# Eight load buffers for the small convolutions, delta u written over u, and ScalarE seeding the sums' bank

## The chip, the cores and the metric

The kernel runs on one core of a Trainium2 chip. A core has five engines that run side by side, each with its own in-order queue: TensorE (matmuls; PE in the profile, with weight loads as PEld), VectorE (DVE), ScalarE (ACT), GpSimd (POOL) and SyncE (SP, which only issues transfers here). All transfers run on 16 DMA engines. The working memory is SBUF, matmuls write to PSUM[...], and scratch tensors lie in device memory (HBM). The metric is the device time of one execution in microseconds, lower is better.

## The reference, cut to what matters

Eight images of 384 channels and 32 x 32 pixels go through four layers. Layer 0 is a state space block over the 1024 pixels in sequence, run forwards and backwards with the same weights and added; with it goes a 3 x 3 convolution per channel. For each direction:

```python
u, z = split(x_norm @ in_proj.T)
u = silu(conv1d(u) + conv1d_b)            # four taps per channel, causal
dt, B, C = split(u @ x_proj.T)            # 24, 16 and 16 columns
delta = softplus(dt @ dt_proj + dt_b)
h = exp(delta * A) * h + (delta * u) * B  # step by step over the pixels, 16 states
y = (C * h).sum(states) + D * u
out = (y * silu(z)) @ out_proj.T
```

Layer 1 has two 1 x 1 convolutions around a 3 x 3 convolution per channel, linear attention and an MLP with GELU. Layers 2 and 3 have depthwise convolutions up to 13 x 13, for which all images are needed at once. Everything is float32.

## The kernel before, in words

**Stages.** Layers 0 and 1 run image by image in `_layers01`; layers 2 and 3 follow for all images together (`conv` in `tile_layers`, lines 282 to 372) and are not touched. For each image b there are three pieces: `front(b)` (lines 572 to 685) prepares the scan's inputs, `scan(b)` (lines 687 to 809) runs the recurrence, `layer1(b)` (lines 869 to 1077) is layer 1. The loop at the end interleaves `scan(b)`, `front(b + 1)` and `layer1(b - 1)`: after each of the scan's 48 rounds it takes as many steps of the other two as their share of cost asks for. Only the first front and the last `layer1` stand alone. The framework hands out buffers and puts the waits in; the order of each engine's queue comes from this interleaving, which the framework's planner may shift where it thinks an operand late.

**The front.** After a normalisation and the input projection, the 3 x 3 convolution (`conv3`, line 532) and the four-tap convolution (line 626 on) load shifted copies of their input from HBM: for each block of 128 channels four tiles of the tag `im`, one for 32 channels, each with three or four shifted copies in the partitions (L541 `lc_i` here and `dw_i` in layer 1, L637 `ut`). Four column groups of TensorE then work on the four tiles (L511). SyncE issues these loads, and in the same queue those of the scan. `N_IM` sets how many such tiles there are: six.

The four-tap convolution of both directions goes through silu into two tiles `uc` of the tag `a6` (L645), one for each direction, with three channel blocks each; seven tiles of that tag serve the whole of layers 0 and 1. For each channel block L666 and L670 then make delta (`dl`), and `deltas`, put off by a step or two, multiplies it with u (L676, into a tile `v` of the tag `t2`), sends both to HBM (L677, L678, on GpSimd's queue), adds the two directions' u (L679) and lets ScalarE scale the sum by D (L681, into `ud`, tag `t2`). `t2` is the general scratch tag of 128 x 512 tiles: eleven buffers, for the squares (L581), the projection's output, delta, v, ud, the MLP's hidden block `hm` (L1054) and others.

**The scan.** A unit is a direction, a half of the pixels and a block of 128 channels: 12 for each image. A unit has four rounds, each for four of the 16 states, and a round has two half rounds. In a half round ScalarE takes two exponentials (`da`, L768, four buffers), VectorE one product (`du`, L773) and two scans (`hs`, L785, eight buffers), and GpSimd one product with C (L794). TensorE sums over the states with a selection matrix, two rounds later (`sums`, line 724): four matmuls of 32 columns each (L728) into one PSUM bank `acc`, of which there is a single one, over the four rounds of a unit. Written in float32, a matmul is two instructions in the profile. In the first round an identity matmul (L733) adds `y0` to the bank: D u in the first direction, and in the second the first direction's result. At a unit's end the bank is copied out by ScalarE (L738) or multiplied with silu(z) by VectorE (L741). `y0`, the copy and z share three buffers of the tag `s2`.

Of the kernel before, what the change touches and what calls it, by code (L numbers as in the profile page):

```python
# [9 lines left out]
AF = mybir.ActivationFunctionType  # L10
# [10 lines left out]
HALF = 512  # L21
# [12 lines left out]
NR = NST // 4  # L34
IMG = (H + 2) * (W + 2)

N_A6, N_T2, N_S2, N_W, N_IM = 7, 11, 3, 4, 6
N_REP, N_DA, N_HS = 6, 4, 8
TP = H * (KP // 2)
PADW = KS // 2  # L40
# [334 lines left out]
def _layers01(tc, nc, B, xv, x2_d, dram, ident, mean_w, eps5, eps6, one, half, minus1, vec, bns, bnt,  # L375
# [12 lines left out]
    with ExitStack() as ctx:  # L388
# [26 lines left out]
        dlv = dl_d.rearrange("b d (c p) l -> b d p c l", p=P)  # L415
        vv = v_d.rearrange("b d (c p) l -> b d p c l", p=P)
# [45 lines left out]
        def t2(name):  # L462
            return sp.tile([P, HALF], FP, tag="t2", name=name, bufs=N_T2)
# [108 lines left out]
        def front(b):  # L572

            xn = []
            for h in range(2):
                cols = bass.ts(h, HALF)
                xh = a6(f"xi_{b}_{h}")
                nc.sync.dma_start(xh, xv[b][:, :, cols])
                sqs = [t2(f"sq_{b}_{c}_{h}") for c in range(NC)]
                for c in range(NC):  # L580
                    nc.scalar.activation(sqs[c], xh[:, c, :], AF.Square)  # L581
                rstd = rsqrt_mean(sqs, eps6, f"ms_{b}_{h}")
                t, mid = image6(f"xn_{b}_{h}")
                for c in range(NC):
                    nc.vector.scalar_tensor_tensor(
                        mid[c], rows(xh[:, c, :]), vec("norm_w", c), rows(rstd), ALU.mult, ALU.mult
                    )
                put_image(xn_d, b % 2, h, t, nc.gpsimd)
                xn.append(mid)
                yield 3  # L590
            uo = u_d[b % 2].rearrange("(c p) i -> p c i", p=P)
            for e in range(2):
                w = wtile(inproj_t[:, e * C : (e + 1) * C], f"win_{b}_{e}")
                for h in range(2):
                    for m in range(NC):
                        ps = psum(f"in_{b}_{e}_{m}_{h}")
                        dense(ps, w, m, xn[h])
                        t = t2(f"uz_{b}_{e}_{h}_{m}")
                        if e == 0:
                            nc.scalar.copy(t, ps)  # L600
                            nc.scalar.dma_start(uo[:, m, 3 + h * HALF : 3 + (h + 1) * HALF], t)
                        else:
                            nc.scalar.activation(t, ps, AF.Silu)
                            nc.scalar.dma_start(zv[b][:, m, bass.ts(h, HALF)], t)
                        yield 3


            t3 = tapw(taps3, f"t3_{b}")
            for h in range(2):
                for c in range(NC):  # L610
                    xr = t2(f"xr_{b}_{h}_{c}")
                    nc.sync.dma_start(xr, xv[b][:, c, bass.ts(h, HALF)])
                    ps = conv3(xn_d, b % 2, h, c, t3, f"lc_{b}_{h}_{c}")
                    lc = t2(f"lg_{b}_{c}_{h}")
                    nc.scalar.activation(lc, ps, AF.Sigmoid, bias=vec("dw_b0", c))

                    def local(h=h, c=c, lc=lc, xr=xr):
                        nc.vector.tensor_mul(rows(lc), rows(lc), xn[h][c])
                        nc.vector.scalar_tensor_tensor(xr, lc, rs, xr, ALU.mult, ALU.add)
                        nc.gpsimd.dma_start(x1v[b][:, c, bass.ts(h, HALF)], xr)  # L620

                    defer(1, local)
                    yield 3


            for h in range(2):
                cols = bass.ts(h, HALF)
                ucs = [a6(f"uc_{b}_{h}_{d}") for d in range(2)]
                for c in range(NC):
                    uts = []  # L630
                    for j in range(4):
                        ut = sp.tile([P, 18 * (W + 2)], FP, tag="im", name=f"ut_{b}_{h}_{c}_{j}", bufs=N_IM)
                        src = bass.AP(
                            u_d.tensor, u_d[b % 2, 32 * (4 * c + j), h * HALF].offset,
                            [[UL, 32], [1, 4], [1, HALF + 3]],
                        )
                        nc.sync.dma_start(ut[:, 0 : HALF + 3], src)  # L637
                        uts.append(ut)
                    for d in range(2):
                        ps = psum(f"c1_{b}_{h}_{c}_{d}")  # L640
                        col32(
                            ps, lambda j, i: t1[:, d * NG + 4 * c + j, :],
                            lambda j, i: uts[j][:, 3 * d : 3 * d + HALF], 1,
                        )
                        nc.scalar.activation(ucs[d][:, c, :], ps, AF.Silu, bias=vec("conv1d_b", c))  # L645
                    yield 2

                xd = t2(f"xd_{b}_{h}")
                ps = psum(f"xd_{b}_{h}")
                for k in range(NC):  # L650
                    for d in range(2):
                        nc.tensor.matmul(
                            ps[64 * d : 64 * d + 64, :], wx[:, k, :], ucs[d][:, k, :],
                            start=(k == 0), stop=(k == NC - 1), skip_group_check=True,
                        )
                nc.scalar.copy(xd, ps)
                for d in range(2):
                    lo = 64 * d + DTR
                    nc.scalar.dma_start(bc_d[b, d][:, cols], xd[lo : lo + 2 * NST, :])
                yield 3  # L660
                for c in range(NC):
                    dls = []
                    for d in range(2):
                        ps = psum(f"dt_{b}_{h}_{d}_{c}")
                        at = slice(64 * d, 64 * d + DTR)
                        nc.tensor.matmul(  # L666
                            ps, wdt[at, c * P : (c + 1) * P], xd[at, :], start=True, stop=True
                        )
                        dl = t2(f"dl_{b}_{h}_{d}_{c}")
                        nc.scalar.activation(dl, ps, AF.Softplus, bias=vec("dt_b", c))  # L670
                        dls.append(dl)

                    def deltas(h=h, c=c, dls=dls, ucs=ucs):
                        for d in range(2):
                            dl, t = dls[d], t2(f"v_{b}_{h}_{d}_{c}")
                            nc.vector.tensor_mul(t, dl, ucs[d][:, c, :])  # L676
                            nc.gpsimd.dma_start(dlv[b, d][:, c, bass.ts(h, HALF)], dl)  # L677
                            nc.gpsimd.dma_start(vv[b, d][:, c, bass.ts(h, HALF)], t)  # L678
                        nc.vector.tensor_add(ucs[0][:, c, :], ucs[0][:, c, :], ucs[1][:, c, :])  # L679
                        ud = t2(f"ud_{b}_{h}_{c}")  # L680
                        nc.scalar.activation(ud, ucs[0][:, c, :], AF.Copy, scale=vec("D", c))  # L681
                        nc.scalar.dma_start(udv[b][:, c, bass.ts(h, HALF)], ud)

                    defer(1, deltas)
                    yield 3

        def scan(b):
# [36 lines left out]
            def sums(k, r, hs, acc, y0, zt):  # L724
                d, h, c = units[k]
                cols = bass.ts(h, HALF)
                for j in range(4):
                    nc.tensor.matmul(  # L728
                        acc[32 * j : 32 * j + 32, :], selt, hs[j // 2][:, bass.ts(j % 2, HALF)],
                        start=(r == 0), stop=(r == NR - 1), skip_group_check=True,  # L730
                    )
                if r == 0:
                    nc.tensor.matmul(acc, ident, y0, start=False, stop=False, skip_group_check=True)  # L733
                if r < NR - 1:
                    return
                if d == 0:
                    yt = s2(f"yt_{b}_{h}_{c}")
                    nc.scalar.copy(yt, acc)  # L738
                    nc.scalar.dma_start(yfv[b][:, c, cols], yt)
                else:  # L740
                    nc.vector.tensor_mul(zt, acc, zt)  # L741
                    nc.gpsimd.dma_start(gv[b][:, c, cols], zt)
# [3 lines left out]
            acc = y0 = zt = nxt = None  # L746
            for k, (d, h, c) in enumerate(units):
                cols = bass.ts(h, HALF)
                second = k % (2 * NC) >= NC
                for r in range(NR):  # L750
                    if r == 0:
                        acc = accp.tile([P, HALF], FP, tag="acc", name=f"acc_{b}_{d}_{h}_{c}")
                        y0 = s2(f"y0_{b}_{d}_{h}_{c}")
# [9 lines left out]
                    for i in range(2):  # L763
                        dlt, vt = now[i]
                        da = sp.tile([P, 2 * HALF], FP, tag="da", name=f"da_{b}_{k}_{r}_{i}", bufs=N_DA)
                        for j in range(2):
# [3 lines left out]
                                scale=neg_a[:, g, r : r + 1],  # L770
# [435 lines left out]
```

## Time and profile before

The time is 5718.41 us, the median of 3 runs (5712.15 to 5722.47). The profiled execution spans 5739.7 us.

| Engine | Busy, us | Share of the span | Instructions |
|---|---|---|---|
| TensorE, matmuls | 4793.9 | 84% | 19550 |
| VectorE | 3602.0 | 63% | 3679 |
| ScalarE | 2886.6 | 50% | 3821 |
| GpSimd | 2872.7 | 50% | 1603 |

| Stage | Stretch, us | TensorE busy | VectorE | ScalarE | GpSimd |
|---|---|---|---|---|---|
| first front alone | 0 to 220 | 118.54 | 24.65 | 49.42 | 56.38 |
| scan of image 1 | 220 to 690 | 296.78 | 414.86 | 274.15 | 319.48 |
| scan of image 4 | 1870 to 2430 | 482.44 | 405.54 | 349.43 | 317.11 |
| scan of image 5 | 2430 to 2990 | 486.50 | 417.17 | 353.77 | 326.72 |
| last `layer1` alone | 4590 to 4960 | 311.25 | 30.12 | 72.32 | 10.72 |
| layers 2 and 3 | 4960 to 5740 | 739.74 | 131.01 | 100.65 | 158.51 |

The page's line of an engine in forty slices has one digit for each slice of 143 us, the busy share in tenths. An answer of waits reads "engine, line, what waited for it": the total in us, how often, and the longest. In the order of time a line has the start, the time taken, engine, source line, operation, output and inputs, the count, and in brackets how long the engine stood idle before it and what let it go. SPq and POOLq are the parts of those engines that issue transfers. Averages over the whole run hide that the stages have different limits, so each is read by itself.

### The profile page before, as it was taken

What the parts mean: (1) busy time and instruction counts of PE and PEld (TensorE: products, weight loads), DVE (VectorE), ACT (ScalarE), POOL (GpSimd) and SP (SyncE); (2) the same over time, 40 slices, a digit from 0 to 9 for tenths busy, and PEclk for the clock granted to TensorE, in tenths of its full rate; (3) what the DMA queues carried; (4) which work ended last, traced back from release to release, by engine and by line L of the source; (5) the groups of instructions that cost most, each with busy time, mean ns of one, the idle gap of its engine ahead of it and who ended that gap; (6) DMA issues with size and microseconds to landing.
All of it is one profiled execution on the core that took longest, in us unless ns stands there. A gap on an engine that the chain in (4) does not pass through costs nothing. (4 is left out here: it accounts for less than half of the span.)

```text
span 5739.7 us, 57345 instructions
## 1 busy us (share of the span) xinstructions
PE 4793.9 (84%) x19550; PEld 2100.7 (37%) x19550; DVE 3602.0 (63%) x3679; ACT 2886.6 (50%) x3821; POOL 2872.7 (50%) x1603
## 2 busy tenths in 40 slices
PE   4666579878898799779888997898878879899899
PEld 1121123322332243224323332332233224597498
DVE  0498887868887668676877785788578701111211
ACT  1555546764676368646774676467636612000211
POOL 3376665647755556565655574557456700110133
PEclk7786689988999899989999998899989989999999
DMA  9655575677567755764565477547644531466676
GB/s 297 220 181 166 175 238 175 224 195 225 175 219 217 208 170 190 173 214 129 182 213 181 139 184 204 171 148 190 180 135 133 128 88 50 105 162 162 192 165 151
DMA packets 528252, 1012.13 MB, mean 176 GB/s; under 512 B 60616, under 2 KB 196248, under 8 KB 527960
## 3 DMA queue, kind: packets, MB, share of 16 engines
q1 hardware_dynamic: 387952, 665.99, 39.2%
q0 software_dynamic: 71136, 248.53, 16.8%
q10 hardware_dynamic: 68872, 93.95, 5.0%
q8 instruction: 155, 2.54, 0.2%
q14 instruction: 137, 1.12, 0.1%
HBM read 763.86 MB, written 288.36 MB: 183 GB/s over the span
## 5 line engine op out<-in xcount | busy, mean ns | idle before, releaser
L794 POOL TENSOR_TENSOR hs<-hs,bct 128x1024 f32<-128x1024 f32 x768 | 2362.9, 3078 | 1160.7 <-DVE hs L785 659.6
L768 ACT ACTIVATE da<-dlt,neg_a 128x512 f32<-128x512 f32 x1536 | 1031.3, 714 | 864.1 <-DVE hs L785 780.0
L785 DVE TENSOR_TENSOR_SCAN hs<-da,carry,du 128x512 f32<-128x512 f32 x768 | 946.8, 1268 | 411.2 <-PE acc L728 228.1
L773 DVE TENSOR_TENSOR du<-vr,bct 128x1024 f32<-128x1024 f32 x768 | 1043.4, 1359 | 121.7 <-DMA vr<-v_d 74.7
L785 DVE TENSOR_TENSOR_SCAN hs<-da,du 128x512 f32<-128x512 f32 x768 | 900.9, 1208 | 187.5 <-ACT da L768 110.9
L728 PE MATMUL acc<-hs,selt 128*32 128x512 f32 x3072 | 725.2, 665 | 271.6 <-POOL hs L794 214.5
L1056 PE MATMUL mo<-hm,w 128*128 128x512 f32 x1152 | 557.3, 623 | 66.1 <-ACT hm L1054 42.9
L502 PE MATMUL mf<-ln,w 128*128 128x512 f32 x1152 | 554.9, 623 | 55.7 <-ACT dl L670 28.9
L768 ACT ACT_TABLE_LOAD x299 | 383.6, 1283 | 30.5 <-DVE hs L785 20.5
L728 PEld LDWEIGHTS acc<-hs,selt 128*32 128x32 f32 x3072 | 124.1, 114 | 683.7 <-POOL hs L794 351.8
L1056 PEld LDWEIGHTS mo<-hm,w 128*128 128x128 f32 x1152 | 213.6, 195 | 400.4 <-issue 242.0
L502 PEld LDWEIGHTS mf<-ln,w 128*128 128x128 f32 x1152 | 218.4, 198 | 381.1 <-issue 297.4
L502 PE MATMUL in<-xn,win 128*128 128x512 f32 x576 | 302.2, 658 | 39.5 <-ACT phi_k L866 35.0
L511 PE MATMUL dw<-dw_i,t3b 96*32 96x512 f32 x1152 | 243.4, 728 | 94.3 <-DMA dw_i<-h_d 94.0
L316 PE MATMUL cv_b<-xt_b,toep 128*64 128x256 f32 x2688 | 305.0, 389 | 14.4 <-DVE xt_b L298 14.4
L316 PE MATMUL cv_a<-xt_a,toep 128*64 128x256 f32 x2688 | 304.2, 388 | 9.2 <-DVE xt_a L298 9.2
L316 PEld LDWEIGHTS cv_b<-xt_b,toep 128*64 128x64 f32 x2688 | 282.6, 199 | 37.2 <-issue 16.8
L316 PEld LDWEIGHTS cv_a<-xt_a,toep 128*64 128x64 f32 x2688 | 282.3, 199 | 30.8 <-issue 10.2
L511 PE MATMUL lc<-lc_i,t 96*32 96x512 f32 x1152 | 218.1, 675 | 61.9 <-DMA lc_i<-xn_d 32.2
L1054 ACT ACTIVATE hm<-mf,biasf 128x512 f32<-128x512 f32 x192 | 131.6, 687 | 169.0 <-PE mf L502 167.4
L502 PE MATMUL op<-g,wo 128*128 128x512 f32 x288 | 149.7, 666 | 76.7 <-issue 42.6
L511 PE MATMUL c<-ut,t 128*32 128x512 f32 x768 | 175.2, 655 | 40.4 <-DMA ut<-u_d 37.7
(184 smaller groups left out, 5296.8 us busy)
## 6 DMA issues: line engine op xcount, KB each, us to landing
dlt<-dl_d SPq DMA_DIRECT2D x384, 256.0 KB, 4.4
vr<-v_d SPq DMA_DIRECT2D x384, 256.0 KB, 4.7
bct<-bc_d SPq DMA_DIRECT2D x256, 256.0 KB, 3.7
ut<-u_d SPq DMA_DIRECT2D x192, 257.5 KB, 5.4
lc_i<-xn_d SPq DMA_DIRECT2D x192, 228.8 KB, 5.0
dw_i<-h_d SPq DMA_DIRECT2D x192, 228.8 KB, 4.2
tp_d<-g_d POOLq DMA_DIRECT2D x64, 672.0 KB, 7.1
w<-w_d SPq DMA_DIRECT2D x64, 576.0 KB, 5.4
```

What stands on the lines that cost most here:

```text
L316: nc.tensor.matmul(ps[2 * H * e : 2 * H * (e + 1), 0:BW], tp[:, 2 * (g % (GB // 2)) + e, :, :, t].rearrange("p c j -> p (c j)"), rhs, star ...
L502: nc.tensor.matmul(ps, w[:, k, m * P : (m + 1) * P], rhs[k] if isinstance(rhs, list) else rhs[:, k, :], start=(k == 0), stop=(k == NC - 1),)
L511: nc.tensor.matmul(ps[32 * j : 32 * j + 32, :], lhs(j, i), rhs(j, i), start=(i == 0), stop=(i == taps - 1), skip_group_check=True,)
L728: nc.tensor.matmul(acc[32 * j : 32 * j + 32, :], selt, hs[j // 2][:, bass.ts(j % 2, HALF)], start=(r == 0), stop=(r == NR - 1), skip_group ...
L768: nc.scalar.activation(da[:, bass.ts(j, HALF)], dlt[:, bass.ts(j, HALF)], AF.Exp, scale=neg_a[:, g, r : r + 1],)
L773: nc.vector.tensor_mul(pairs(du), pairs(vt), bct[r][:, 0:1, :].to_broadcast([P, 2, HALF]),)
L785: nc.vector.tensor_tensor_scan(t[:, s][:, way], da[:, s][:, way], du[:, s][:, way], k_c if second else 0.0, ALU.mult, ALU.add,)
L794: nc.gpsimd.tensor_mul(pairs(t), pairs(t), bct[r][:, 1:2, :].to_broadcast([P, 2, HALF]))
L1054: nc.scalar.activation(hm, ps, AF.Gelu, bias=biasf[:, NC * i + f, :])
L1056: nc.tensor.matmul(acc[m], wb[:, f, m * P : (m + 1) * P], hm, start=(i == 0 and f == 0), stop=(i == FF // C - 1 and f == NC - 1),)
```

## The change

Three edits, which share the same memory: two tiles of 2048 bytes a partition go and two of 2448 come.

- The convolutions' loads get eight buffers and not six, enough for two whole convolutions. The scratch tag `t2` gives up two, from eleven to nine.
- delta u is written over u in the tile `uc`, and the store to HBM reads it there; no tile `v` is taken. As u is then gone, the sum of the two directions' u is taken first, into the tile `ud`, which ScalarE scales in place.
- D u (or the first direction's result) reaches the sums' bank by a ScalarE copy ahead of the selection matmuls, which then all add to the bank. The identity matmul stays in the very first unit alone, with the start flag, ahead of the selection matmuls.

```diff
-N_A6, N_T2, N_S2, N_W, N_IM = 7, 11, 3, 4, 6
+N_A6, N_T2, N_S2, N_W, N_IM = 7, 9, 3, 4, 8
...
                     def deltas(h=h, c=c, dls=dls, ucs=ucs):
+                        ud = t2(f"ud_{b}_{h}_{c}")
+                        nc.vector.tensor_add(ud, ucs[0][:, c, :], ucs[1][:, c, :])
                         for d in range(2):
-                            dl, t = dls[d], t2(f"v_{b}_{h}_{d}_{c}")
-                            nc.vector.tensor_mul(t, dl, ucs[d][:, c, :])
-                            nc.gpsimd.dma_start(dlv[b, d][:, c, bass.ts(h, HALF)], dl)
-                            nc.gpsimd.dma_start(vv[b, d][:, c, bass.ts(h, HALF)], t)
-                        nc.vector.tensor_add(ucs[0][:, c, :], ucs[0][:, c, :], ucs[1][:, c, :])
-                        ud = t2(f"ud_{b}_{h}_{c}")
-                        nc.scalar.activation(ud, ucs[0][:, c, :], AF.Copy, scale=vec("D", c))
+                            v = ucs[d][:, c, :]
+                            nc.vector.tensor_mul(v, dls[d], v)
+                            nc.gpsimd.dma_start(dlv[b, d][:, c, bass.ts(h, HALF)], dls[d])
+                            nc.gpsimd.dma_start(vv[b, d][:, c, bass.ts(h, HALF)], v)
+                        nc.scalar.activation(ud, ud, AF.Copy, scale=vec("D", c))
                         nc.scalar.dma_start(udv[b][:, c, bass.ts(h, HALF)], ud)
...
             def sums(k, r, hs, acc, y0, zt):
                 d, h, c = units[k]
                 cols = bass.ts(h, HALF)
+                if r == 0 and b == 0 and k == 0:
+
+                    nc.tensor.matmul(acc, ident, y0, start=True, stop=False, skip_group_check=True)
+                elif r == 0:
+                    nc.scalar.copy(acc, y0)
                 for j in range(4):
                     nc.tensor.matmul(
                         acc[32 * j : 32 * j + 32, :], selt, hs[j // 2][:, bass.ts(j % 2, HALF)],
-                        start=(r == 0), stop=(r == NR - 1), skip_group_check=True,
+                        start=False, stop=(r == NR - 1), skip_group_check=True,
                     )
-                if r == 0:
-                    nc.tensor.matmul(acc, ident, y0, start=False, stop=False, skip_group_check=True)
                 if r < NR - 1:
                     return
                 if d == 0:
```

## The prediction

> **What bounds the kernel now.** I read the page's slices first, then a table of 100 us stretches, then the waits of each engine, and last the order of time at two places.
>
> ```profile
> PE   4666579878898799779888997898878879899899
> DVE  0498887868887668676877785788578701111211
> ACT  1555546764676368646774676467636612000211
> ```
>
> Forty slices of 143 us. The last eight belong to the large convolutions, which this change does not touch. From slice 2 to 32 (220 to 4590 us) the scan of eight images runs beside other work. In its first image (220 to 690 us) VectorE is full (414.86 us busy of 470) and TensorE is not (296.78), so VectorE sets the pace. In each later image, some 560 us long, TensorE is busy for about 486 us and VectorE for about 420: neither is full over the whole image.
>
> ```profile
> 2000.00:2100.00 100.00, 97.17 (x346) 46.73 (x345) 60.24 (x52) 56.75 (x87) 51.42 (x28) 0.98 0.47 151
> 2400.00:2500.00 100.00, 71.26 (x231) 26.77 (x230) 71.43 (x86) 52.05 (x75) 56.81 (x39) 0.85 0.77 187
> 2600.00:2700.00 100.00, 96.98 (x319) 39.95 (x318) 66.97 (x62) 66.89 (x93) 53.39 (x21) 0.93 0.44 133
> 2800.00:2900.00 100.00, 88.59 (x262) 29.37 (x257) 84.09 (x76) 73.09 (x87) 68.70 (x34) 0.95 0.65 200
> ```
>
> The columns are TensorE, its weight loads, VectorE, ScalarE, GpSimd, the granted clock, the DMA share and GB/s. About four of the six stretches of an image look like the first, third and fourth rows (TensorE 88 to 97%, the bound); the start of an image looks like the second: nobody is full, and waits set the time. These are the waits that the change touches:
>
> ```profile
> PE dw L511 <- DMA dw_i<-h_d: 94.0, 41, 9.9
> PE c L511 <- DMA ut<-u_d: 37.7, 21, 11.1
> PE lc L511 <- DMA lc_i<-xn_d: 32.2, 11, 10.2
> PE mf L502 <- ACT dl L670: 28.9, 6, 7.0
> PE mf L502 <- ACT uc L645: 22.0, 7, 5.0
> PE acc L728 <- ACT yt L738: 28.4, 10, 7.2
> PE acc L728 <- DVE zr L741: 28.4, 16, 6.7
> ```
>
> The numbers are total us, times and the longest. The first three are TensorE waiting for convolution loads (163.9 us), the next two for ScalarE, the last two for the one bank of the sums to come free.
>
> [...] The trace has 562 to 587 ns for the sums' copy on L738; that is used. [...] in the trace no copy line carries a table load. [...] the multiply on L676 takes 660 ns at least and 2856 at most.
>
> **Part 1, the identity matmul (L733).**
>
> ```profile
> L733 PE MATMUL acc<-y,ident x192: 592/697/1222, 233.0 to 4576.3; 128*128 128x512 f32 x192
> ```
>
> Each of the 96 is two instructions; 95 pairs go. The timeline around 2319 us has a pair at 2318.95 and the next matmul at 2320.01, so one is worth 1.06 us of TensorE: 95 x 1.06 = 101 us. The first image holds 11 of them under a full VectorE, worth nothing there; 84 x 1.06 = 89 us lie in images two to eight. TensorE sets the pace in about 0.6 of those: **-53 us** (ends 0 and -89).
>
> In their place stand 95 ScalarE copies of 0.585 us (L738's median), 56 us. ScalarE is half busy and sits 780.0 us before the exponentials of L768 waiting for VectorE, so I cost the copies' own time at nothing. The new waits are another matter. The copy must wait for the bank: ahead of it in ScalarE's queue, in direction 0, is its own copy out (L738); in direction 1 it waits for VectorE's multiply on L741. Queued behind it are the exponentials and the evictions of the other layers. The exponentials are up to four tiles ahead of the scan, so a wait of one half round (3.8 us from scan to scan at 2500 us) starves nobody. On the other side the four sums matmuls now wait for ScalarE to reach the copy. Where TensorE already waits for the bank today (10 + 16 times in the list above) it will wait longer: 0.6 us more for the copy in the 16, and in the 10 also for up to two exponential pairs of 1.33 us: 16 x 0.6 + 10 x 3.3 = 43 us of TensorE, mostly at the starts of images where it is not full: **+20 us** (ends 0 and +43; if ScalarE is late in many more of the 95 units, 95 x 1 us more).
>
> **Part 2, eight load buffers.** A convolution takes four loads. With six buffers the third and fourth load of the next convolution wait until the one before has been computed, and a load lands some 4 us after its issue. At 2503.72 us SyncE issues six loads, from then on four at a time as TensorE lets go. With eight, two whole convolutions are in flight. SyncE's queue is in order, and behind a held load stand the scan's own: SyncE waits 200.9 us for L541 on lc, 135.4 on dw, 116.3 for L637, and VectorE loses 74.7 us to late vr and, between 1270 and 4115 us, 25.9 us to late bct loads. Of the 163.9 us of TensorE waits 105.7 lie between 600 and 4580 us (76.0 + 25.4 + 4.3); half of that comes through to the end, since VectorE is 70 to 85% busy there: -50. The first 220 us run at a DMA share of 0.85 and gain little, the last image's own convolution after 4590 us about 10, its 9.9 us wait: **-60 us** (ends -20 and -110).
>
> **Part 3, delta u in the place of u, and the sum first.**
>
> ```profile
> 2339.98 3.44 DVE L676 TENSOR_TENSOR v<-dl,uc 128x512 f32<-128x512 f32 x2
> 2343.34 0.68 DVE L679 TENSOR_TENSOR uc<-uc,uc 128x512 f32<-128x512 f32 x1
> 2344.05 0.72 ACT L681 ACTIVATE ud<-uc,pk 128x512 f32<-128x512 f32 x1 [6.86 <-DVE uc L679]
> 2346.82 2.84 PE L502 MATMUL mf<-ln,w 128*128 128x512 f32 x6 [3.63 <-ACT uc L645]
> 2348.84 1.28 DVE L785 TENSOR_TENSOR_SCAN hs<-da,carry,du 128x512 f32<-128x512 f32 x1 [3.63 <-ACT da L768]
> ```
>
> ScalarE's D u (L681) stands in its in-order queue until VectorE has done two multiplies and the sum; TensorE (3.63 us) and the scan (3.63 us) then wait for what is queued behind it. With the sum first, ScalarE is let go two multiplies earlier: 3.4 us here, 2 x 0.96 = 1.9 us by the mean L676 between 600 and 4580 us. 37 such waits x 1.9 = 70 of the 120.6 us that L681 waits. What reaches TensorE are the waits of L502 mf above, 28.9 + 22.0 = 51 us; half of them: **-25 us** (ends 0 and -70). The instructions themselves stay the same in number and shape: nothing.
>
> **Part 4, nine scratch tiles and not eleven.** The deltas take 3 scratch tiles a block and not 5, so nine last three blocks and eleven lasted 2.2. At the turn of an image this matters:
>
> ```profile
> 1273.13 0.61 ACT L581 ACTIVATE sq<-xi 128x512 f32<-128x512 f32 x1
> 1283.64 0.54 POOL L678 DMA_DIRECT2D v_d<-v  x1 [10.28 <-DMA x_d<-xx]
> 1295.70 0.63 ACT L581 ACTIVATE sq<-xi 128x512 f32<-128x512 f32 x1 [21.95 <-DMA ud_d<-ud]
> 1296.97 1.22 DVE L785 TENSOR_TENSOR_SCAN hs<-da,du 128x512 f32<-128x512 f32 x1 [23.05 <-ACT da L768]
> ```
>
> The second square finds no scratch tile until stores leave, the stores stand in GpSimd's queue, which is held by the stores of x_d, and ScalarE holds the scan 23.05 us. Three squares and one more tile after 15 delta tiles in 11 need 8 of them back; after 9 in 9 they need 4. The stall stays in part, since GpSimd is held as before. ScalarE's square waits are 41.5 + 19.2 us: **-20 us** (ends 0 and -45). Against it: everywhere else two tiles fewer, and u's tiles, seven for all users, are held until the store of v has landed and not only until the sum; the load of the next image stands behind that in SyncE's queue. No row shows either; between 0 and one landing of some 5 us at each of 7 turns: **+10 us** (ends 0 and +40).
>
> **Sum.** -53 + 20 - 60 - 25 - 20 + 10 = -128 us. The waits overlap: a stall that TensorE loses in part 2 or 3 lets it run into VectorE, 75% busy, sooner. I take 0.8 of it, -103: 5718 - 103 = **5615 us**.
>
> **Rivals.**
> (a) Another engine takes over. VectorE loses no work; an image is some 560 us with VectorE at 420 us busy, 465.81 and 481.55 in the second and third. Then waits only change hands (TensorE's from loads and ScalarE to GpSimd's product on L794, today 214.5 us) and a third of the sum is left, -43, with part 1's new waits at their upper end (23 more): about 5698. For it: in the first image this is so already. Against it: four stretches in six have TensorE at 88% or more.
> (b) The stalls are chains, and taking the head of each frees all engines at once: the parts at two thirds of their far ends, (89 + 110 + 70 + 45) x 2/3 = 209, less 30 for the new waits: about 5540. For it: at 2348 and 1297 us TensorE, VectorE and ScalarE stand together. Against it: the DMA share of 0.6 to 0.7 bounds how much earlier loads can land.
> (c) Slower. ScalarE late at the copies in all 95 units (95 x 1 us), u's tiles and scratch at their ends (+40), and only half of the gains of parts 2 to 4 (-52) and a third of part 1 (-18), with the 43: -52 - 18 + 95 + 40 + 43 = +108; at half of that, about 5770. For it: ScalarE's queue is in order and carries table loads (1283 ns) between the exponentials and the other layers' functions, and it is 70 to 80% busy in the later half of an image, so it can be behind TensorE there. Against it: TensorE is behind all others in just that half.
>
> **How the numbers follow.** Forecast 0.58, (a) 0.18, (b) 0.12, (c) 0.12. Faster by over 0.2% (11 us): forecast, (b) and most of (a), 0.84; within it: the rest of (a) and the mild end of (c), 0.05; slower 0.11. The range has the forecast, half of (b) and all but the end of (a): 5540 to 5705.
>
> **What would show each step.** Part 1: the row of L733 at 2 instructions, a new ScalarE copy row of 95 near 0.6 us, TensorE's busy time down by about 100 us, and a new wait of L728 for that copy of 30 to 60 us; over 100 us there would speak for (c). Part 2: waits of L511 for loads from 164 to under 60 us, those of L773 for vr and bct down too. Part 3: L681's wait from 120.6 to about 50 us, mf's waits for ScalarE halved. Part 4: no square at a turn waits over 15 us. The large convolutions after 4960 us keep their 780 us. The prediction is wrong if these waits go and L728's wait for L794, or the scan's for ScalarE, grows by the same sum.

## The result, and the profile after

The changed kernel takes 5570.95 us (median of 4 runs, 5550.92 to 5587.58) against 5720.44 us for the kernel before on the same chip: ratio 0.9734, 95% interval 0.9695 to 0.9773. Measured once more beside other kernels it was 0.9721 (0.9702 to 0.9740), 5565.27 against 5721.04 us. So some 150 us went, where 103 were forecast; the time lies inside the range given, between the forecast and rival (b). The profiled executions span 5739.7 us before and 5548.9 us after. The first is the longest execution on record of its kernel and the second the shortest of its own, so differences between these two traces add up to 191 us, some 40 more than the medians show. Line numbers from 675 on have moved: the scan is L788 (was L785), the exponentials L771 (L768), GpSimd's product L797 (L794), the sums L733 (L728), VectorE's closing product L744 (L741); L731 is the new ScalarE copy.

The page's slices of the changed kernel, 139 us each:

```profile
PE   5665589868996899689978987898698799899899
DVE  1598997967787778687977896788788601111211
ACT  1565546774686368646774776477546422001211
```

The picture is the old one: VectorE full in the first image, nobody full over a later one. The fifth image, from the last closing product of the fourth to that of the fifth, in a table of stretches (columns as in the prediction), of the kernel before:

```profile
2405.00:2972.00 567.00, 490.05 (x1720) 179.06 (x1720) 424.19 (x422) 356.62 (x460) 328.75 (x156) 0.92 0.60 177
```

and of the changed one:

```profile
2325.00:2866.00 541.00, 456.54 (x1696) 170.95 (x1696) 426.50 (x420) 358.07 (x469) 328.17 (x155) 0.92 0.61 184
```

26 us less for one image in these two traces. TensorE's busy time is 33 us less, VectorE's and GpSimd's the same, and TensorE is busy 84% of the stretch, not more than the 86% before. Over the run, the first front alone went from 217.55 to 196.34 us (the first product of the scan), the scans together from 4366.4 to 4209.9 us, and the last `layer1` alone from 390.1 to 377.2 us (from the last closing product to the first large convolution); layers 2 and 3 kept their 765 us. In the trace of the second measurement, which spans 5567.0 us, the scans took 4228 us: of the three differences that of the scans is the one to be taken as rough, while the first front takes 214 to 219 us in the traces of all kernels with six load buffers and 193 to 199 us in those with eight.

TensorE's waits in the changed kernel that answer to the seven shown before:

```profile
PE dw L511 <- DMA dw_i<-h_d: 38.6, 15, 9.6
PE c L511 <- DMA ut<-u_d: 18.4, 4, 12.3
PE lc L511 <- DMA lc_i<-xn_d: 8.8, 7, 3.3
PE mf L502 <- ACT uc L645: 27.9, 7, 11.7
PE mf L502 <- ACT dl L670: 11.0, 2, 8.3
PE acc L733 <- ACT acc L731: 20.2, 5, 10.8
```

The loads: 65.8 us in place of 163.9. ScalarE ahead of mf: 38.9 in place of 50.9. The bank (`acc`, 128 x 512 values of PSUM): 20.2 us for the copy in place of 28.4 + 28.4 for the two that free the bank, so TensorE's new wait is smaller than the ones it replaced, also with the 10.9 us for the copy that stand at the MLP's second matmul (L1059); ScalarE in its turn now waits for the bank before the copy, 25.5 us for VectorE's closing product and 4.8 us for its own copy out. The copy itself, in the view by source line, and what held ScalarE ahead of it:

```profile
L731 ACT COPY acc<-y x95: 573/589/602, 256.1 to 4397.5; 128x512 f32<-128x512 f32 x95
  DVE zr L744: 25.5, 12
```

ScalarE's wait for the sum of the two u:

```profile
ACT ud L681 <- DVE ud L675: 88.5, 22, 14.9
```

It was 120.6 us in 37. And the turn from the second to the third image, in order of time, which answers to the four lines at 1273 us:

```profile
1216.98 1.67 ACT L581 ACTIVATE sq<-xi 128x512 f32<-128x512 f32 x3 [0.96 <-ACT ud L681]
...
1224.94 0.54 POOL L680 DMA_DIRECT2D v_d<-uc  x1 [6.58 <-DMA x_d<-xx]
...
1236.73 1.28 ACT L560 ACT_TABLE_LOAD   x1 [16.85 <-DMA ud_d<-ud]
...
1242.79 2.06 DVE L585 SCALAR_TENSOR_TENSOR xn<-xi,pk,ms_b 128x512 f32<-128x512 f32 x3 [18.75 <-PE ms_b L564]
```

The squares no longer look for a scratch tile and run at once. But the next step of the same normalisation (L560) also takes a scratch tile, and there ScalarE stands 16.85 us for the store of ud; TensorE and, for 18.75 us, VectorE wait for what follows from it. GpSimd is held by the stores of x_d as before. So the stall moved by one step and became a little shorter (it was 21.95 us). Over the whole run ScalarE waited 31.8 us for stores to give a scratch tile back, all of it on L560; before it was 60.7 us on the squares and 23.4 us on L670, 84.1 in all.

### The profile page after: what moved, and what is told of

Read it like the earlier page. It is cut to its first block, busy times and chain, and to the rows that moved or that the text cites. A ratio compares the mean times of both kernels' runs of the same rounds, so it can differ in the third digit from the quotient of the medians.

```text
span 5548.9 us, 57079 instructions
## 1 busy us (share of the span) xinstructions
PE 4603.1 (83%) x19360; PEld 2057.3 (37%) x19360; DVE 3614.0 (65%) x3679; ACT 2906.8 (52%) x3902; POOL 2888.6 (52%) x1603
## 5 line engine op out<-in xcount | busy, mean ns | idle before, releaser
L797 POOL TENSOR_TENSOR hs<-hs,bct 128x1024 f32<-128x1024 f32 x768 | 2377.3, 3097 | 1078.2 <-DVE hs L788 600.5
L771 ACT ACTIVATE da<-dlt,neg_a 128x512 f32<-128x512 f32 x1536 | 1031.0, 714 | 759.0 <-DVE hs L788 716.1
L788 DVE TENSOR_TENSOR_SCAN hs<-da,carry,du 128x512 f32<-128x512 f32 x768 | 946.5, 1268 | 327.8 <-ACT da L771 161.5
L776 DVE TENSOR_TENSOR du<-vr,bct 128x1024 f32<-128x1024 f32 x768 | 1057.2, 1377 | 85.8 <-DMA vr<-v_d 50.2
L788 DVE TENSOR_TENSOR_SCAN hs<-da,du 128x512 f32<-128x512 f32 x768 | 898.6, 1207 | 80.2 <-ACT da L771 36.2
L733 PE MATMUL acc<-hs,selt 128*32 128x512 f32 x3072 | 668.9, 657 | 263.6 <-POOL hs L797 235.4
L1059 PE MATMUL mo<-hm,w 128*128 128x512 f32 x1152 | 569.4, 636 | 89.5 <-ACT hm L1057 64.0
L502 PE MATMUL mf<-ln,w 128*128 128x512 f32 x1152 | 549.8, 619 | 38.9 <-ACT uc L645 27.9
L1059 PEld LDWEIGHTS mo<-hm,w 128*128 128x128 f32 x1152 | 216.1, 198 | 432.2 <-issue 243.5
L733 PEld LDWEIGHTS acc<-hs,selt 128*32 128x32 f32 x3072 | 111.7, 113 | 671.6 <-POOL hs L797 395.5
L511 PE MATMUL dw<-dw_i,t3b 96*32 96x512 f32 x1152 | 211.6, 611 | 39.0 <-DMA dw_i<-h_d 38.6
L511 PE MATMUL lc<-lc_i,t 96*32 96x512 f32 x1152 | 199.8, 656 | 38.3 <-issue 29.0
L298 DVE COPY xt_b<-xt_b 64x2480 f32<-64x2480 f32 x24 | 38.2, 1594 | 263.1 <-DMA xt_b<-xp_d 263.1
```

What stands on the lines that cost most here:

```text
L298: nc.vector.tensor_copy(half1[:, :, 0 : XL - 1], half0[:, :, 1:XL])
L502: nc.tensor.matmul(ps, w[:, k, m * P : (m + 1) * P], rhs[k] if isinstance(rhs, list) else rhs[:, k, :], start=(k == 0), stop=(k == NC - 1),)
L511: nc.tensor.matmul(ps[32 * j : 32 * j + 32, :], lhs(j, i), rhs(j, i), start=(i == 0), stop=(i == taps - 1), skip_group_check=True,)
L733: nc.tensor.matmul(acc[32 * j : 32 * j + 32, :], selt, hs[j // 2][:, bass.ts(j % 2, HALF)], start=False, stop=(r == NR - 1), skip_group_ch ...
L771: nc.scalar.activation(da[:, bass.ts(j, HALF)], dlt[:, bass.ts(j, HALF)], AF.Exp, scale=neg_a[:, g, r : r + 1],)
L776: nc.vector.tensor_mul(pairs(du), pairs(vt), bct[r][:, 0:1, :].to_broadcast([P, 2, HALF]),)
```

## The experiments

**The parts alone, at six load buffers.** First each part by itself on the kernel before, four kernels on one chip (before: 5723.67 us). The ScalarE seed alone:

```diff
+                if r == 0 and b == 0 and k == 0:
+                    nc.tensor.matmul(acc, ident, y0, start=True, stop=False, skip_group_check=True)
+                elif r == 0:
+                    nc.scalar.copy(acc, y0)
...
-                        start=(r == 0), stop=(r == NR - 1), skip_group_check=True,
+                        start=False, stop=(r == NR - 1), skip_group_check=True,
...
-                if r == 0:
-                    nc.tensor.matmul(acc, ident, y0, start=False, stop=False, skip_group_check=True)
```

> The kernel before with the ScalarE seed alone (eleven scratch tiles, six load buffers, the old deltas). If the parts add as in the prediction's sum, part 1 gives -53 + 20 = -33 us, ratio about 0.994. If TensorE's time comes through in full (the bound in most of the scan, and the new wait as small as the 20 us of the trace after), -80 us, 0.986. If the in-order ScalarE queue pays for it, 1.00 or above.

Measured: 0.9994 (0.9985 to 1.0002). Its page:

```profile
PE 4671.9 (82%) x19360; PEld 2068.5 (36%) x19360; DVE 3634.1 (64%) x3679; ACT 2910.9 (51%) x3899; POOL 2873.6 (50%) x1603
```

122 us of TensorE's busy time are gone and the time has not moved. Either ScalarE paid for it, or TensorE was not what bounded; the pair of kernels that leave the seed out, below, bears on it.

The load buffers alone:

```diff
-N_A6, N_T2, N_S2, N_W, N_IM = 7, 11, 3, 4, 6
+N_A6, N_T2, N_S2, N_W, N_IM = 7, 9, 3, 4, 8
```

> The kernel before with eight load buffers and nine scratch tiles alone. The prediction's part 2 gives -60 us, less the cost of two scratch tiles under the old, hungrier deltas (+10 to +40): between -50 and -20 us, ratio 0.991 to 0.997. If TensorE's waits for loads come through one for one (98 us fewer in the trace after), -90 us, 0.984. If scratch tiles are what counts, no gain or a loss, since 15 delta tiles now meet nine buffers.

Measured: 0.9796 (0.9775 to 0.9818), 117 us. This one line is most of the change. The first front alone, in the kernel before,

```profile
0.00:217.00 217.00, 116.89 (x391) 34.81 (x395) 22.30 (x69) 47.38 (x65) 56.38 (x109) 0.77 0.85 273
```

and with eight buffers:

```profile
0.00:196.00 196.00, 109.14 (x393) 34.74 (x397) 22.21 (x69) 43.77 (x61) 56.44 (x109) 0.79 0.95 303
```

The last two columns are the DMA share and GB/s: the same bytes (217 us x 273 and 196 us x 303 GB/s are both 59 MB) in 21 us less, with the DMA share at 0.95 in place of 0.85. Here there is no scan whose loads could be held, so the gain is the convolutions' own. The scans together took 4255.5 us (111 less), the last `layer1` 377.3 (13 less). These two traces differ by 145 us where the medians differ by 117 to 121, so for the scans some 85 to 111 us is as much as can be said. TensorE's waits for convolution loads fell to 55.0 us:

```profile
PE dw L511 <- DMA dw_i<-h_d: 33.2, 10, 10.0
PE c L511 <- DMA ut<-u_d: 13.3, 3, 7.7
PE lc L511 <- DMA lc_i<-xn_d: 8.5, 7, 3.3
```

SyncE's own waits for load buffers (L541 and L637), behind which the scan's loads stand, fell from 452.6 to 322.9 us. And the convolutions' matmuls, the same number of them, kept TensorE busy for 549.6 us in place of 636.7. For the 3 x 3 convolution of layer 1, before and with eight buffers (busy time and mean ns of one stand after the bar), and then its shortest, median and longest matmul before:

```profile
L511 PE MATMUL dw<-dw_i,t3b 96*32 96x512 f32 x1152 | 243.4, 728 | 94.3 <-DMA dw_i<-h_d 94.0
L511 PE MATMUL dw<-dw_i,t3b 96*32 96x512 f32 x1152 | 206.4, 614 | 33.7 <-DMA dw_i<-h_d 33.2
L511 PE MATMUL dw<-dw_i,t3b x1152: 589/592/1063, 784.3 to 4698.3; 96*32 96x512 f32 x192
```

The median is 592 ns with either number of buffers; what changed is how many are slow. Before, 299 of the 1152 took over 1000 ns, and with eight buffers 41, every one of them while the trace's record of the granted clock stands at half speed (0.5 of full); all those near 592 ns ran at full speed. In the kernel before the clock fell to half 118 times after the first 250 us; in the 3.4 us ahead of a fall (the shortest stretch of the record) TensorE was busy for 26% (median), ahead of a rise for 100%. From these figures the author's estimate is that late loads cost twice here: TensorE stands still (94.0 us for the loads of dw before, 33.2 with eight), and more of the matmuls that come next are at half speed (299 for 41). No run changes the one without the other. For the four-tap convolution it is another thing: its matmuls are no shorter (663 ns for 655), but more of its four column groups run side by side, 3.5 matmuls at a time (768 x 663 ns over 145.2 us busy) in place of 2.9 (768 x 655 ns over 175.2 us).

The new deltas alone (the `deltas` of the diff, with eleven scratch tiles and six load buffers):

> The kernel before with the new deltas alone (sum first, delta u over u; eleven scratch tiles, six load buffers). The prediction's parts 3 and 4 give -25 - 20 + a few = about -40 us, ratio 0.993. If the trace after is the measure, where ScalarE's wait on the sum only fell from 120.6 to 88.5 us, -15 us, 0.997. If the longer hold of u's tiles costs, 1.00 or above.

Measured: 1.0016 (1.0007 to 1.0025), slightly slower. The last kernel of the four takes only the sum ahead and leaves delta u in a tile of its own:

```diff
+                        ud = t2(f"ud_{b}_{h}_{c}")
+                        nc.vector.tensor_add(ud, ucs[0][:, c, :], ucs[1][:, c, :])
                         for d in range(2):
                             dl, t = dls[d], t2(f"v_{b}_{h}_{d}_{c}")
...
-                        nc.vector.tensor_add(ucs[0][:, c, :], ucs[0][:, c, :], ucs[1][:, c, :])
-                        ud = t2(f"ud_{b}_{h}_{c}")
-                        nc.scalar.activation(ud, ucs[0][:, c, :], AF.Copy, scale=vec("D", c))
+                        nc.scalar.activation(ud, ud, AF.Copy, scale=vec("D", c))
```

> As the one before, but delta u still goes to a scratch tile of its own: only the sum is taken ahead of the two multiplies. If the order on VectorE is what counts in part 3, it equals the in-place kernel, 0.993 to 0.997. If the scratch tiles are what counts (the stall at an image's turn), it stays within 0.2% of the kernel before.

Measured: 1.0054 (1.0041 to 1.0066), slower by 31 us, for which no theory had a place. ScalarE is let go earlier (L681 waits 86.5 us in the in-place kernel and 99.2 in this one, before 120.6), but what it runs into next is late: its waits for the scan's loads of delta were 35.5 us before, 84.8 in place, and with only the sum first

```profile
ACT da L768 <- DMA dlt<-dl_d: 90.0, 20, 16.2
```

Why these loads come later was not tried; the same wait is 80.4 us in one of the kernels below that is faster than before, so it is a candidate and no more. In the in-place kernel ScalarE's waits for stores to free a scratch tile all but went (9.1 us, before 84.1), as part 4 had it, and the time did not fall.

**The parts taken back, at eight load buffers.** These four kernels ran on another chip than the others (before: 5684.92 us), and the changed kernel did not run there, so they are compared with it by ratios alone. The identity matmuls put back into the changed kernel (the first diff of this section reversed):

> The changed kernel with the identity matmuls put back, so load buffers and new deltas together. If the ScalarE seed is worth nothing at eight load buffers either (as it was at six: ratio 0.9994), it equals the changed kernel, 0.973. If the seed pays once the loads no longer hold the queue, it stays at about the load buffers' own 0.980.

Measured: 0.9793 (0.9780 to 0.9806). The old deltas put back into the changed kernel:

> The changed kernel with the old deltas, so load buffers, nine scratch tiles and the ScalarE seed. If the new deltas' worth is to make nine scratch tiles enough, this is slower than the changed kernel by 20 to 40 us, ratio about 0.979. If they are worth nothing, 0.973. If the seed does not pay either, 0.980, as the load buffers alone.

Measured: 0.9781 (0.9767 to 0.9794). Either part taken back leaves about the worth of the load buffers alone. For the first this was found again on the changed kernel's chip, below; for the old deltas it rests on the two chips' ratios. Next the two scratch tiles by themselves, `N_T2` from 11 to 9 in the kernel before:

> The kernel before with nine scratch tiles and nothing else changed, six load buffers. If scratch tiles are short under the old deltas, slower by 10 to 40 us, 1.002 to 1.007; the load buffers' own worth is then the 0.9796 measured with nine tiles less this. If the two tiles never bind, 1.000.

Measured: 1.0021 (1.0011 to 1.0031), 12 us. Last, one step further, `N_T2, N_IM = 7, 10` in the changed kernel:

> The changed kernel taken one step on: ten load buffers and seven scratch tiles. If the loads' hold on SyncE's queue is still what binds (TensorE still waits 65.8 us for convolution loads), another -20 to -50 us, ratio 0.965 to 0.970. If two whole convolutions in flight are all that is needed, 0.973. If seven scratch tiles bind, 0.98 or worse.

Measured: 0.9775 (0.9761 to 0.9788), with 55.7 us of TensorE's waits for loads left, 10 less than the changed kernel: no better than eight and nine. Two convolutions in flight are enough, or what seven scratch tiles cost eats what ten buffers bring; this run does not part the two.

**Nothing in the place of the seed.** Four kernels on one chip (before: 5721.04 us). The changed kernel and the one with the identity matmuls back once more, and the kernel before and the changed one with neither identity matmul nor copy, the first selection matmul carrying the start flag; these two leave D u and the first direction's result out.

```diff
-                if r == 0:
-                    nc.tensor.matmul(acc, ident, y0, start=False, stop=False, skip_group_check=True)
```

> The changed kernel once more, beside the three below on one chip. Its first ratio was 0.9734 (0.9695 to 0.9773). If the parts add up beyond the load buffers, it stays near 0.973; if the load buffers are the whole of it, it comes to 0.979, as the kernels with the seed or the new deltas taken back.

Measured: 0.9721 (0.9702 to 0.9740).

> The changed kernel with the identity matmuls put back, once more (0.9793 before). If the ScalarE seed pays at eight load buffers, this is slower than the changed kernel beside it by 0.3% or more; if not, equal within the intervals.

Measured: 0.9802 (0.9785 to 0.9820). Beside each other on one chip with intervals that do not touch, the kernel with the ScalarE seed is faster by 0.8%, 45 us, when the new deltas and eight load buffers are there.

> The kernel before with nothing added to the sums' bank: the identity matmuls are left out and no copy takes their place, so D u and the first direction's result are missing from the output (y0 is still loaded). If TensorE bounds 0.6 of the later images, as the prediction took it, -53 us, ratio 0.991, and the seed kernel's 0.9994 then means that the ScalarE copies cost what the matmuls saved. If TensorE is not what bounds at six load buffers, 0.999 to 1.001, and the copies cost nothing.

Measured: 1.0001 (0.9990 to 1.0012). Its page, and what TensorE waits for most:

```profile
PE 4708.6 (82%) x19358; PEld 2068.3 (36%) x19358; DVE 3653.9 (64%) x3679; ACT 2872.7 (50%) x3813; POOL 2884.6 (50%) x1603
```

```profile
PE acc L728 <- POOL hs L792: 275.5, 113, 15.5
```

85 us of TensorE's busy time taken out for nothing, and the wait for GpSimd's product, 214.5 us before, grew by 61. So at six load buffers TensorE's work is not time, although it is 88 to 97% busy in four stretches of six; and as the seed kernel measures the same, the ScalarE copies cost nothing there that the time shows.

The clock comes into it too, which the prediction left out. The identity matmuls had kept TensorE busy for 127.4 us, but only 85 came off: the other matmuls took 42 us more. The granted clock was 0.891 to 0.896 in all 13 executions of this kernel, and 0.897 to 0.904 in the 17 of the kernel before beside it; in the traces the clock stands at half speed for 1246 us, before for 1117. The same shows wherever the identity matmuls are gone: 0.886 to 0.895 in the seed kernel (1226 us at half speed), and at eight load buffers 0.896 to 0.899 in the changed kernel for 0.903 to 0.907 with them back. Whether their removal would have brought time at an unchanged clock, no run here tells.

> The changed kernel with nothing added to the sums' bank, so D u and the first direction's result are missing from the output. Against the changed kernel beside it this is the price of the ScalarE copies at eight load buffers: if they are hidden, equal; if ScalarE's queue pays for them, faster by up to 95 x 0.6 = 56 us, 1%. Against the kernel with the identity matmuls back it is the price of those: -53 us if TensorE bounds 0.6 of the images, nothing if it does not.

Measured: 0.9836 (0.9820 to 0.9853). Neither expectation: with less to do than either, it is slower than the changed kernel by 1.2% and than the one with the identity matmuls by 0.3%. Its waits at the bank and for ScalarE (L739 and L736 are its closing product and its copy out):

```profile
PE mf L502 <- ACT dl L670: 52.1, 6, 13.2
PE acc L728 <- DVE zr L739: 49.9, 10, 10.9
PE acc L728 <- ACT yt L736: 28.1, 11, 4.8
```

78.0 us at the bank. In the nine kernels without the ScalarE seed these two waits add up to 40 to 78 us; in the five with it TensorE waits 9.5 to 22.8 us for the copy. So the seed does take most of TensorE's wait for the free bank away; ScalarE waits for the bank instead, 29 to 57 us in these five.

A comparison of the queues says more. Of the 9295 matmuls that this kernel and the changed one share, 3917 stand at another place of TensorE's queue, 262 of them by more than 20 places; of 3402 computing and issuing instructions of ScalarE, 1836. In the seed kernel against the kernel before it is 3867 of 9680 and 1829 of 3530. (Table loads are left out; only their order tells them apart.) So no single edit here is a change of one cost: each also moved other work in the queues, mostly by a few places.

## Why the prediction was right, and where not

**The whole.** Direction and range held; the size was 150 us for a forecast of 103. That the sum came so near is in part luck: the load buffers brought twice their forecast, parts 1 and 3 brought nothing by themselves, and these errors offset each other. The sign of being wrong that the prediction named was not seen in the changed kernel: TensorE's wait for GpSimd's product grew by 21 us only (214.5 to 235.4), and the scan's wait for ScalarE fell from 241.9 to 197.7.

**Part 2, the load buffers: mechanism right, size too small.** Forecast -60 us, ends -20 and -110. Measured -117 with nine scratch tiles, which by themselves cost 12; if the two add, which no run shows, about -129, beyond the far end. Two terms were mis-sized. The first front was to "gain little" at a DMA share of 0.85; it gained 21 us of 217, as the share went to 0.95. (The last `layer1` gained 13 us, forecast about 10.) And "half of that comes through" was wrong for the scans: 105.7 us of waits were counted, and some 85 to 111 us came. The sum had no term for what late loads do to the matmuls themselves, 87 us of busy time in the convolutions, of which the slow clock is a part (dw alone: 299 slow matmuls before, 41 with eight buffers); how much of it reached the time is not shown. The forecast fall of the scan's own load waits on VectorE came with the buffers alone (vr and bct 37.4 us, before 100.6) but less so in the changed kernel (74.6); with nine scratch tiles and six load buffers it was 55.3, so this wait also moves with the order of the queues. How much of the gain went through SyncE's held queue and how much through TensorE was not separated; the first front shows that it is not all the queue.

**Part 1, the identity matmul: the step failed.** It said that TensorE sets the pace in about 0.6 of images two to eight, -53 us. Alone, the removal is worth nothing, with the copies (0.9994) and without (1.0001). Without the copies the wait for GpSimd's product grew, as rival (a) had named. With them it did not (217.8 us); there TensorE waited longer for ScalarE at mf (60.2 us for uc, before 22.0). In both the clock stood at half speed for longer (1246 us without the copies and 1226 with them, before 1117). A share of 88 to 97% busy was not evidence of a bound; which of these things took the saved work's place is open. The second step, +20 us for longer waits of TensorE at the bank, had the wrong sign: 56.8 us became 20.2, or 31.1 with those at L1059. That the copies' own 56 us are hidden under ScalarE's idle time agrees with the two equal times at six load buffers.

**Part 3, the sum first: the step failed by itself.** The wait on L681 was to fall to about 50 us and bring 25; it fell to 88.5. Alone the sum first costs 0.5%, and together with delta u over u 0.2%; in both traces ScalarE met later loads.

**Part 4: mechanism right, no gain by itself.** The squares' waits for stores, 60.7 us, went to nothing, as said (with the old deltas at nine tiles they stand on L681 instead, 60.3 us), and a stall of 16.85 us stayed at the same turn, at the fourth scratch tile of the count. But with the new deltas and all eleven tiles these waits were gone too, and the time was 0.2% longer and not 20 us shorter. Two scratch tiles fewer under the old deltas cost 12 us; the +10 of the prediction was for the new deltas, and no run measures it.

**A reading.** Rival (a) takes VectorE's 465.81 and 481.55 us in the second and third image against an image of 560 us. They are of stretches of 580 and 600 us: VectorE is about 80% busy there, not 83 to 86%.

**What is open.** Load buffers, seed and new deltas together give 0.9721 to 0.9734; load buffers with either of the others 0.978 to 0.980, and load buffers alone 0.9796. The last 0.5 to 0.8% thus come only with seed and deltas together, at eight buffers. Three candidates stand. The bank wait of TensorE is shorter, but with the old deltas it is as short (19.4 us) and gains nothing that the intervals show. ScalarE waits less for scratch tiles (31.8 us; with the old deltas at nine tiles about 80), but without the seed it waits nearly as little (38.4 us) and the kernel is no faster than with the load buffers alone. The third is the new order of the queues, which was never changed by itself; that two edits which add no work were slower by 0.5% (the sum ahead) and, against the identity matmuls, by 0.3% (nothing in the place of the seed) leaves room for it. The runs do not settle which.

Rivals (b) and (c): the time lies some 60% of the way from the forecast to (b), but by the load buffers and not by all heads of the chains; of (c), the late copies were not seen.

## What to carry to other kernels

A loader that feeds groups of four tiles wants whole groups in flight: six buffers left half a group waiting for the group before, and two more were worth 2%, most of it in the scans. Look at the spread of one matmul's durations too: a median of 592 ns beside a mean of 728 was the mark of a quarter of them running at half clock. Before costing an engine's saved work as time, take that work out and look: 85 us less of an engine that is 84% busy were worth nothing here. And where a planner lays out the queues, an edit is to be measured in the kernel it will live in: two parts that were worth nothing alone made it 0.5 to 0.8% faster together, for a reason that stayed open.

## What the runs showed of the hardware

A ScalarE copy of 128x512 float32 from SBUF into PSUM took 589 ns (573 to 602, L731 of the changed kernel), about as long as one out of PSUM into SBUF (585 ns, 562 to 587, L738 of the kernel before). In all 95 units the matmuls that follow carry no start flag. That they add to what ScalarE wrote was the author's assumption: a trace shows the order of the work and not the sums, so no run here shows it.

The granted clock of TensorE took two values in the traces, full and half (1.0 and 0.5). In the kernel before, a matmul of the dw convolution (512 columns) took 592 ns in the median, at full speed, and up to 1063 ns at half speed; 299 of its 1152 were slow, and 41 with eight load buffers. In that same kernel, after the first 250 us, the clock fell 118 times to half; in the 3.4 us ahead of a fall TensorE was busy for 26% (median), ahead of a rise for 100% (median). Without the identity matmuls the mean granted clock was 0.006 to 0.010 lower than in the kernel with them that ran beside it (four pairs: 0.891 and 0.893 for 0.901 at six load buffers, 0.897 and 0.899 for 0.905 at eight).
